# Layer 0: the second half's normalisers in steps inside the first half's attention loop, and state sums row by row

## The chip, the cores and the metric

One core of a Trainium2 chip runs the kernel, a network of four layers, in one launch. The metric is the device time of a run in microseconds. Before the change it was 4101.22 us, the median of three runs (4100.05 to 4104.15).

The engines named below: PE multiplies matrices into PSUM, DVE, ACT and POOL work on vectors, SP issues most of the transfers between SBUF and DRAM. Each of them works through its own queue of instructions in order, and waits for others by semaphores.

## The reference, cut to what matters

Only layer 0 is touched. It is a linear attention over windows of a 64 x 64 image, with 8 heads of 32 channels (d, f below) and three window sizes. `norm` is the normaliser that this change is about: the sum of k over a window, times q, summed over the 32 channels of a head.

```python
q = sigmoid(q); k = sigmoid(k)
v = v / maximum(norm(v, axis=1), 1e-12)
Ik = _integral(k)                       # running sums over rows and columns
Ikv = _integral(einsum('bfhw,bghw->bfghw', k, v))
for w in (1, 2, 4):
    ws = 64 // w
    wk = _box(Ik, ws, 64, 64)           # window sums: four corners of Ik
    wkv = _box(Ikv, ws, 64, 64)
    attn = einsum('bdhw,bdfhw->bfhw', q, wkv)
    norm = einsum('bdhw,bdhw->bhw', q, wk)
    outs.append((attn / (norm[:, None] + 1e-06)).reshape(b, C, 64, 64))
x = x + einsum('bchw,oc->bohw', concatenate(outs, 1), Wout) + bout
```

Layers 1 to 3 (a deformable convolution, a gated linear attention with a mixture of experts, a softmax attention with another) follow and stay as they were.

## The kernel before

The 256 channels are split in two halves of 128 (4 heads each). A tile is 8 x 16 positions (128), 32 tiles in all, 8 rows of 4. Layer 0 has two stages.

**The front** (`layer0`, up to the second group of pools). For each half `hf`: `project0` makes q, k (as 128 channels x 4096), v and, for each tile, the state S = k v; `sums0` adds states of neighbouring tiles on POOL (`near`: rows up to one apart; `S`: up to three rows and one column apart), after all eight rows are there; `norms0` makes the normalisers. `norms0` copies k block by block to `T` (ACT), scans along image rows (DVE), adds down the rows inside a block (7 additions) and from block to block (7), which gives the integral image. Then, for three windows and eight blocks, it makes a product: `d`, a difference of rows of T (DVE), `e`, a difference of columns (a copy on ACT, one or two subtractions on DVE: the middle L433 and the edge L435), and `pr` = e x q (DVE, L437). A matmul with `head_at` sums the channels of each head (L439); all 24 products of a half accumulate into one PSUM bank of 96 rows. At the end DVE takes the reciprocal, and SP stores it to DRAM as `recd`. Tiles `d`, `e`, `prq` have two buffers.

**The loop** (`half0` and `region0`, for both halves one after the other). It computes the attention as masked scores. A half is 224 jobs: for each of two halves of the image 28 jobs for the far tiles, and then for each of four output rows I 4 jobs of the far columns and 12 to 20 near ones. A job is four score matmuls, one per head (L549, into six PSUM banks that are used in turn), whose results are multiplied by a mask and go to SBUF: two heads by DVE (L559), two by ACT (a copy, L555) and POOL (the mask, L565). Two jobs later PE multiplies them with v into accumulators (L592). PE's order in the loop is written out by the program (`manual_schedule`); the order on the other engines is found by a scheduler from the program's dependences.

After a row, `out_rows` multiplies the accumulators by the reciprocals (L616, L628, L629), which were loaded from `recd` over SP with each row broadcast to 32 partitions (L477), projects them (L144, `l_x_ps`) and adds them to x, which was loaded as `xs` (two buffers, L624) and is stored to `xd` (L641). In the first half each row also clears 4160 KB of a list `xs` in DRAM that a later layer uses (`clear_list`: DVE makes zeros, L1553, SP stores them, L1555). `self.later` is a list of small pieces of work, one of which is done per job.

Pools are stacks of memory: the loop's tiles take the space of the front's, so the loop's first instructions wait for the last ones that read the front's tiles.

Of the kernel before, what the change touches and what calls it, by code (L numbers as in the profile page):

```python
# [19 lines left out]
P = 128  # L20
# [66 lines left out]
class Net:  # L87
# [141 lines left out]
    def consts0(self, pool):  # L229
        nc = self.nc  # L230

        self.head_at = pool.tile([P, NBLK, 4 * NBLK], F32, tag="head_at", name="head_at")
        nc.gpsimd.memset(self.head_at, 0.0)
        for h in range(4):
            flat = self.head_at[h * D : (h + 1) * D].rearrange("p a b -> p (a b)")
            nc.gpsimd.memset(flat[:, h : h + 36 * (NBLK - 1) + 1 : 36], 1.0)

        self.gate = pool.tile([P, TR, HW], F32, tag="gate", name="gate")
        nc.gpsimd.memset(self.gate, 1.0)
        nc.gpsimd.memset(self.gate[:, :, 0:1], 0.0)  # L240
# [51 lines left out]
    def layer0(self, xc, x, xd, done):  # L292
# [4 lines left out]
        with tc.tile_pool(name="l0", bufs=1) as pool, tc.tile_pool(name="l0d", bufs=1, space=DRAM) as dpool:  # L297
            q = [pool.tile([P, N], F32, tag=f"q{hf}", name=f"l0_q{hf}") for hf in range(2)]
            k = [pool.tile([P, N], F32, tag=f"k{hf}", name=f"l0_k{hf}") for hf in range(2)]
# [3 lines left out]
            recd = dpool.tile([2, 3 * D, NB], F32, tag="recd", name="l0_recd")  # L303
            with tc.tile_pool(name="l0m", bufs=1) as tmp:
                M = self.masks0(pool, tmp)
            with tc.tile_pool(name="l0y", bufs=1) as ypool:
                self.consts0(ypool)
                y = ypool.tile([P, 2, N], F32, tag="y", name="l0_y")
                tiled = lambda a: a.rearrange("p (i u r c) -> p i r u c", i=NBLK, u=NU, r=TR)
                raster = lambda a: a.rearrange("p (i r u c) -> p i r u c", i=NBLK, r=TR, u=NU)  # L310
                self.group_norm(xc, lambda m: [(tiled(y[:, m])[:, i], raster(xc[:, m])[:, i]) for i in range(NBLK)])
                done()
                with (
                    tc.tile_pool(name="l0g", bufs=1) as gpool,
                    tc.tile_pool(name="l0a", bufs=2) as wp,
                    tc.tile_pool(name="l0a_ps", bufs=2, space=PSUM) as ps,
                ):
                    self.weights(ypool, ["w_qk0", "w_kv0"])
                    for hf in range(2):
                        self.project0(hf, y, q[hf], k[hf], v[hf], S[hf], wp, ps)  # L320
                        self.sums0(S[hf], near[hf], gpool)
                        self.norms0(q[hf], k[hf], recd[hf], gpool, wp, ps)
            with (
# [9 lines left out]
                self.later, self.second = [], []  # L333
                with tc.manual_schedule(engines={mybir.EngineType.PE}):
                    for hf in range(2):
                        self.half0(hf, q[hf], k[hf], v[hf], S[hf], near[hf], recd[hf], M, bd, x, xd, st, wp, ps)
                    for go in self.second:
                        go()
                    while self.later:
                        self.later.pop(0)()  # L340
# [4 lines left out]
    def project0(self, hf, y, q, k, v, S, wp, ps):  # L345

        nc, w = self.nc, self.w
# [7 lines left out]
        for nb in range(NBLK):  # L355
# [24 lines left out]
            for h in range(4):  # L380
                hp = slice(h * D, (h + 1) * D)
                (nc.scalar.copy if h % 2 else nc.vector.tensor_copy)(S[hp, ts, :], p[hp, :, hp])

    def sums0(self, S, near, pool):


        nc = self.nc
        I8 = lambda a: a.rearrange("p (i j) e -> p i j e", j=4)
        R = pool.tile([P, NT, D], F32, tag="R", name="l0_R")
        f32, r, s4 = I8(near), I8(R), I8(S)  # L390
        add = lambda o, a: nc.gpsimd.tensor_tensor(o, o, a, ALU.add)
        nc.gpsimd.tensor_copy(near, S)
        add(f32[:, 1:], s4[:, :-1])
        add(f32[:, :-1], s4[:, 1:])
        nc.gpsimd.tensor_copy(R, near)
        for d in (2, 3):
            add(r[:, d:], s4[:, :-d])
            add(r[:, :-d], s4[:, d:])
        nc.gpsimd.tensor_copy(S, R)
        add(s4[:, :, 1:], r[:, :, :-1])  # L400
        add(s4[:, :, :-1], r[:, :, 1:])

    def norms0(self, q, k, recd, pool, wp, ps):
# [3 lines left out]
        T = pool.tile([P, HW + 1, HW], F32, tag="T", name="l0_T")  # L407
        nc.gpsimd.memset(T[:, 0, :], 0.0)
        k5 = k.rearrange("p (i u r c) -> p i r u c", i=NBLK, u=NU, r=TR)
        flat = lambda a: a.rearrange("p r x -> p (r x)")  # L410
        rows = T[:, 1:].rearrange("p (i r) x -> p i r x", r=TR)
        for i in range(NBLK):
            nc.scalar.copy(rows[:, i].rearrange("p r (u c) -> p r u c", c=HC), k5[:, i])
            nc.vector.tensor_tensor_scan(flat(rows[:, i]), flat(self.gate), flat(rows[:, i]), 0.0, ALU.mult, ALU.add)
        add = lambda o, a: nc.vector.tensor_tensor(o, o, a, ALU.add)
        for r in range(1, TR):
            add(rows[:, :, r], rows[:, :, r - 1])
        for i in range(1, NBLK):
            add(rows[:, i], bc(rows[:, i - 1, TR - 1], 1, TR))
        p = ps.tile([P, NB], F32, tag="nrm", name="l0_nrm_ps", bufs=1)  # L420
        for wi, ws in enumerate(WINS):
            half, ni = ws // 2, ws // 2 // TR
            a, b = half + 1, HW - half + 1
            for i in range(NBLK):

                d = T[:, TR * (i + ni) : TR * (i + ni + 1)] if i + ni < NBLK else bc(T[:, HW], 1, TR)
                if i >= ni:
                    hi, d = d, wp.tile([P, TR, HW], F32, tag="d", name="l0_d")
                    nc.vector.tensor_tensor(d, hi, T[:, TR * (i - ni) : TR * (i - ni + 1)], ALU.subtract)
                e = wp.tile([P, TR, HW], F32, tag="e", name="l0_e")  # L430
                nc.scalar.copy(e[:, :, :a], d[:, :, half - 1 : half - 1 + a])
                if b > a:
                    nc.vector.tensor_tensor(e[:, :, a:b], d[:, :, a + half - 1 : b + half - 1], d[:, :, a - half - 1 : b - half - 1], ALU.subtract)  # L433
                at = max(a, b)
                nc.vector.tensor_tensor(e[:, :, at:], bc(d[:, :, HW - 1], 2, HW - at), d[:, :, at - half - 1 : HW - half - 1], ALU.subtract)  # L435
                pr = wp.tile([P, NU, TR, HC], F32, tag="prq", name="l0_prq")
                nc.vector.tensor_tensor(pr.rearrange("p u r c -> p r u c"), e.rearrange("p r (u c) -> p r u c", c=HC),  # L437
                                        q[:, i * NB : (i + 1) * NB].rearrange("p (u r c) -> p r u c", u=NU, r=TR), ALU.mult)
                nc.tensor.matmul(p[wi * D : (wi + 1) * D, :], self.head_at[:, i, :], pr.rearrange("p u r c -> p (u r c)"),  # L439
                                 start=(i == 0), stop=(i == NBLK - 1))  # L440
        rec = pool.tile([3 * D, NB], F32, tag="rec", name="l0_rec")
        nc.vector.tensor_scalar_add(rec, p[: 3 * D], 1e-6)
        nc.vector.reciprocal(rec, rec)
        nc.sync.dma_start(out=recd, in_=rec)
# [85 lines left out]
    def region0(self, full, jobs, k, v, wp, ps, after):  # L530
# [68 lines left out]
        for i in range(len(jobs)):  # L599
            done = first(i)  # L600
            if self.later:
                self.later.pop(0)()
            self.second.append((lambda i, done: lambda: second(i, *done))(i, done))
# [3 lines left out]
    def out_rows(self, hf, I, accs, o64, rcp, x, xd, st, wp, ps, part):  # L607
# [13 lines left out]
        if part == 0:  # L621
            self.xs0 = wp.tile([P, 2, NB], F32, tag="xs", name="l0_xs")
# [1585 lines left out]
```

## Time and profile before

| | |
|---|---|
| median of the runs | 4101.22 us (4100.05 to 4104.15) |
| the profiled execution | 4099.97 us, of which its span is 4098.3 |
| mean granted PE clock | 0.927 of full speed |
| busy over the whole span | PE 87%, DVE 42%, ACT 31%, POOL 35% |
| front of layer 0 (first projection to first mask) | 29.1 to 263.5 us |
| first half's loop, to about | 700 us |
| second half's loop, to about | 1055 us |
| the other layers | 1055 to 4098 us |

In the stage of 263.5 to 1055 us PE is busy for 780.24 us of 791.5. In layers 1 to 3 nothing is changed. The page names L565 (POOL, 769.9 us over the two layers that use such lines), L559 (DVE, 492.2) and L555 (ACT, 367.5) as its costliest groups; these are the masks of the loop.

A busy engine is not always the one that sets the end, so the views to read are: busy time by stage; in a stage, what the busiest engine waits for; and the timeline around the place in question.

### The profile page before, as it was taken

Reading aid. Unit: us, or ns where it says so; the run is one execution under the profiler, and the core shown is the slowest. Engines: PE = TensorE matmul, PEld = TensorE weight load, DVE = VectorE, ACT = ScalarE, POOL = GpSimd, SP = SyncE. Lnnn points to the kernel's source line nnn. Section 1 sums busy time; section 2 is a strip of 40 time slices with the busy share of each in tenths; the row PEclk is TensorE's granted clock in tenths of the full one; section 3 lists DMA queues with packets and bytes.
Section 4 is the critical chain, followed back from the end, with each engine's and each line's share of the span. In section 5 each row is a group of like instructions: output and inputs, shape, how many; then the busy total and the mean of one; then the engine's idle time right before and its main releaser. Section 6 shows DMA issues by size and latency. Waiting matters only on the chain.

```text
span 4098.3 us, 57080 instructions
## 1 busy us (share of the span) xinstructions
PE 3563.3 (87%) x21872; PEld 2338.6 (57%) x21872; DVE 1738.9 (42%) x4404; ACT 1267.3 (31%) x2588; POOL 1445.4 (35%) x1376
## 2 busy tenths in 40 slices
PE   7879999999977767656678797999999999799997
PEld 4423433333335656544456575666666668688886
DVE  6876656565653554556566557011011101211111
ACT  4424343434423535311112234122222212233331
POOL 1258898888952243433334341000000001111110
PEclk9989999999998978878778798999999999899999
DMA  1003414210023111110001484000000000455554
GB/s 52 2 26 109 126 57 136 58 39 33 26 94 109 51 44 49 44 30 0 1 11 43 137 259 145 0 10 1 11 11 11 11 11 14 167 193 192 191 190 174
DMA packets 137792, 294.09 MB, mean 72 GB/s; under 512 B 14817, under 2 KB 72802, under 8 KB 128290
## 3 DMA queue, kind: packets, MB, share of 16 engines
q1 hardware_dynamic: 113138, 234.80, 17.7%
q0 software_dynamic: 13056, 35.93, 2.3%
q10 hardware_dynamic: 11312, 19.55, 1.4%
q8 instruction: 178, 2.92, 0.3%
q14 instruction: 108, 0.88, 0.1%
HBM read 202.53 MB, written 87.70 MB: 71 GB/s over the span
## 4 chain that ended last, share of the span: by engine, by line
PE 35%; issue 11%; DVE 5%; POOL 3%; DMA 2%; ACT 1%; SPq 0%; ACTq 0%; POOLq 0%; DVEq 0%
PE a_o_ps L1945 11%; PE a_s_ps L144 11%; PE f_h_ps L144 2%; PE a_qkv_ps L144 2%; PE f_y_ps L144 2%; POOL ys L1782 2%; DMA ys<-f_y,f_at 1%; PE a_q_ps L144 1%; DVE a_sm L1309 1%; PE tr_ps L217 1%; DMA f_g<-ys 1%; PE a_o_ps L144 1%; PE a_u_ps L144 1%; PE a_c_ps L1334 1%; POOL a_tmp L1165 0%
## 5 line engine op out<-in xcount | busy, mean ns | idle before, releaser
L565 POOL TENSOR_TENSOR l_sm<-l_sc,mask 128x512 f32<-128x512 f32 (+3 forms) x624 | 769.9, 1268 | 119.5 <-ACT l_sc L555 117.4
L559 DVE TENSOR_TENSOR l_sm<-l_s,mask 128x256 f32<-128x256 f32 (+3 forms) x1248 | 492.2, 447 | 302.7 <-PE l_s L549 292.9
L555 ACT COPY l_sc<-l_s 128x384 f32<-128x384 f32 (+3 forms) x896 | 367.5, 461 | 558.9 <-PE l_s L549 537.1
L1945 PE MATMUL a_o_ps<-a_v,a_e 128*128 128x257 f32 x2048 | 489.2, 380 | 0.0
L144 PE MATMUL a_s_ps<-a_qT,a_nT 128*128 128x512 f32 (+1 forms) x1152 | 487.8, 546 | 0.0
L1945 PEld LDWEIGHTS a_o_ps<-a_v,a_e 128*128 128x128 f32 x2048 | 388.9, 190 | 147.0 <-issue 103.8
L549 PE MATMUL l_s<-l_q,l_k 32*128 32x384 f32 (+2 forms) x3584 | 423.8, 514 | 7.1 <-ACT l_sc L555 4.1
L1641 POOL DMA_INDIRECT xs<-f_n,f_to x64 | 62.4, 975 | 883.6 <-DVE f_to L1638 840.9
L1940 ACT ACTIVATE a_e<-a_s_ps 128x512 f32<-128x512 f32 (+1 forms) x288 | 158.0, 549 | 687.3 <-PE a_s_ps L144 687.2
L144 PE MATMUL f_h_ps<-f_xT,f_w 128*128 128x256 f32 x1440 | 344.1, 387 | 15.2 <-ACT f_h L1755 5.5
L1782 POOL DMA_INDIRECT ys<-f_y,f_at x144 | 139.6, 970 | 571.3 <-ACT f_y L1781 545.4
L144 PE MATMUL f_y_ps<-f_w,f_h 128*128 128x256 f32 x1440 | 328.1, 379 | 0.0
L144 PEld LDWEIGHTS f_h_ps<-f_xT,f_w 128*128 128x128 f32 x1440 | 264.8, 191 | 83.7 <-ACT f_h L1755 31.5
L854 PE MATMUL l_acc_ps<-ident,l_pr 128*128 128x128 f32 x1600 | 208.9, 291 | 117.8 <-DVE l_pr L850 114.1
L549 PEld LDWEIGHTS l_s<-l_q,l_k 32*128 32x128 f32 x3584 | 164.6, 183 | 240.6 <-issue 123.2
L144 PEld LDWEIGHTS a_s_ps<-a_qT,a_nT 128*128 128x128 f32 x1152 | 216.3, 190 | 129.9 <-issue 112.9
L144 PEld LDWEIGHTS f_y_ps<-f_w,f_h 128*128 128x128 f32 x1440 | 268.2, 190 | 33.7
L854 PEld LDWEIGHTS l_acc_ps<-ident,l_pr 128*128 128x128 f32 x1600 | 193.8, 151 | 132.7 <-DVE l_pr L850 126.4
L850 DVE TENSOR_TENSOR l_pr<-l_vk,l_w_ps 128x1280 f32<-128x1280 f32 x128 | 182.1, 1480 | 91.0 <-ACT l_w_ps L839 79.8
L1755 ACT ACTIVATE f_h<-f_h_ps,f_w 128x256 f32<-128x256 f32 x360 | 163.7, 468 | 131.9 <-PE f_h_ps L144 131.9
L592 PE MATMUL l_a_ps<-l_sm,l_v 128*32 128x512 f32 (+3 forms) x1408 | 179.0, 530 | 1.6 <-POOL l_sm L565 1.5
L592 PE MATMUL l_b_ps<-l_sm,l_v 128*32 128x256 f32 (+2 forms) x2176 | 172.4, 376 | 0.5 <-POOL l_sm L565 0.5
(441 smaller groups left out, 4357.6 us busy)
## 6 DMA issues: line engine op xcount, KB each, us to landing
f_w<-in_f_w SPq DMA_DIRECT2D x36, 1152.0 KB
f_w<-in_f_w SPq DMA_DIRECT2D x36, 1028.0 KB
xs<-zero SPq DMA_DIRECT2D x8, 4160.0 KB
l_vk<-vt SPq DMA_DIRECT2D x180, 128.0 KB
f_x<-xs SPq DMA_DIRECT2D x72, 260.0 KB
f_w<-in_f_w SPq DMA_DIRECT2D x36, 384.0 KB
l_rcp<-l_recd SPq DMA_DIRECT2D x48, 256.0 KB
f_w<-in_f_w SPq DMA_DIRECT2D x36, 257.0 KB
```

What stands on the lines that cost most here:

```text
L144: self.nc.tensor.matmul(out, lhsT, rhs, start=(i == 0), stop=(i == len(pairs) - 1))
L549: nc.tensor.matmul(s[pair, j], k[hp, key * P : (key + 1) * P], qs[hp], start=True, stop=True)
L555: nc.scalar.copy(sc[:, j], s[1, j])
L559: nc.vector.tensor_tensor(sms[0][:, j, at : at + t * wide].rearrange("p (t n) -> p t n", n=wide), part[:, which, :], mask, ALU.mult)
L565: nc.gpsimd.tensor_tensor(sms[1][:, :, at : at + t * wide].rearrange("p j (t n) -> p j t n", n=wide), part[:, :, which, :], bc(mask, 1, 2) ...
L592: nc.tensor.matmul(out, v[:, key, hp], sms[pair][:, j, base + lo * wide : base + hi * wide], start=not seen[nm], stop=(left[nm] == 0 and h ...
L850: nc.vector.tensor_tensor(pr, vk, bc(wps[:, j, dy], 3, D), ALU.mult)
L854: nc.tensor.matmul(acc[:, m, j, :], pf[:, dx, m * P : (m + 1) * P], self.ident, is_transpose=True, start=(j == 0 and dy == 0 and dx == 0 a ...
L1755: nc.scalar.activation(h[:, m, :], q, AF.Gelu, bias=w1[:, 2 * hidden + m : 2 * hidden + m + 1])
L1782: nc.gpsimd.indirect_dma_start(out=self.ys_parts[(i % 4) * NI + k], in_=y[:, k, :], in_offset=None, out_offset=bass.IndirectOffsetOnAxis(a ...
L1940: nc.scalar.activation(e, p, AF.Exp, scale=1.0 / 16.0)
L1945: nc.tensor.matmul(o[i][:, : C + 1], e[:, i * P : (i + 1) * P], v[:, j, :], start=(j == 0), stop=(j == NT - 1))
```

## The change

Four things are done together.

- `norms0` becomes a list of steps: 8 scans, 14 additions, 25 steps that each finish one product (`total`) and make the next (`product`), and `invert`. For half 0 all of them are called in the front. For half 1 the eight scans are called in the front; the other steps are called from `region0` in the loop, one every fourth job, and two more after them.
- Half 1's T takes the place of its k (`kz`): k is copied to DRAM (`kd`) first and loaded again at the end of the steps.
- The head sum of a product is no longer accumulated over 24 products in one bank: each goes to 4 rows of its own bank (in the loop one of the six banks of the scores), is copied back into the first four rows of `pr` by ACT and stored to DRAM (`sumd`) by SP. `invert` loads all 96 rows, takes the reciprocal and stores it. `d`, `e` and `prq` have one buffer each, as has `xs` of the loop. The gate of the scan is bf16 and 128 x 512.
- `sums0` is called after each row of states, and adds what that row completes.

Its core as a diff:

```diff
@@ layer0
+            kz = pool.tile([P, HW + N], F32, tag="kz", name="l0_kz")
+            k = [pool.tile([P, N], F32, tag="k0", name="l0_k0"), kz[:, HW:]]
...
                     for hf in range(2):
-                        self.project0(hf, y, q[hf], k[hf], v[hf], S[hf], wp, ps)
-                        self.sums0(S[hf], near[hf], gpool)
-                        self.norms0(q[hf], k[hf], recd[hf], gpool, wp, ps)
+                        self.project0(hf, y, q[hf], k[hf], v[hf], S[hf], near[hf], gpool, wp, ps)
+                        if hf == 0:
+                            T = gpool.tile([P, HW + N], F32, tag="T", name="l0_T")
+                            for go in self.norms0(q[0], k[0], T, sumd[0], recd[0], wp, lambda: ps.tile([P, NB], F32, tag="nrm", name="l0_nrm_ps", bufs=1)):
+                                go()
+                        else:
+                            nc.sync.dma_start(out=kd, in_=k[1])
+                            for go in self.norms0(q[1], k[1], kz, sumd[1], recd[1], wp, None)[:NBLK]:
+                                go()
...
+                self.slow = self.norms0(q[1], k[1], kz, sumd[1], recd[1], wp,
+                                        lambda: ps.tile([P, 4, P], F32, tag="s", name="l0_nrm_ps", bufs=6).rearrange("p a b -> p (a b)"))[NBLK:]
+                self.slow.append(lambda: nc.sync.dma_start(out=k[1], in_=kd))
+                self.turn = 0
@@ project0, after the states of block nb
+            self.sums0(nb, S, near, R)
@@ sums0, for row I
+        add(near[:, I], S[:, I], S[:, I - 1])
+        add(near[:, I - 1], near[:, I - 1], S[:, I])
+        lo = max(0, I - 3)
+        add(R[:, lo:I], R[:, lo:I], bc(S[:, I], 1, I - lo))
...
+        if I >= 3:
+            done = slice(I - 3, I - 2) if I < NBLK - 1 else slice(I - 3, NBLK)
+            nc.gpsimd.tensor_copy(S[:, done], R[:, done])
+            add(S[:, done, 1:], S[:, done, 1:], R[:, done, :-1])
+            add(S[:, done, :-1], S[:, done, :-1], R[:, done, 1:])
@@ norms0
+        room = lambda nm: wp.tile([P, TR, HW], F32, tag=nm, name=f"l0_{nm}", bufs=1)
+        def scan(i):
...
+            e = room("e")
+            nc.scalar.copy(e.rearrange("p r (u c) -> p r u c", c=HC), k5[:, i])
...
+            nc.vector.tensor_tensor_scan(flat(rows[:, i]), self.gate, flat(e), 0.0, ALU.mult, ALU.add)
...
+        def total(wi, i):
+            p, pr = bank(), made["pr"]
+            nc.tensor.matmul(p[:4], self.head_of, pr, start=True, stop=True)
+            nc.scalar.copy(pr[:4], p[:4])
+            nc.sync.dma_start(out=sumd[wi * D + 4 * i : wi * D + 4 * i + 4, :], in_=pr[:4])
+
+        def invert():
+            rec = room("d").rearrange("p r x -> p (r x)")[: 3 * D]
+            nc.sync.dma_start(out=rec, in_=sumd)
+            nc.vector.tensor_scalar_add(rec, rec, 1e-6)
+            nc.vector.reciprocal(rec, rec)
+            nc.sync.dma_start(out=recd, in_=rec)
+
+        steps = [call(scan, i) for i in range(NBLK)]
+        steps += [call(down, r) for r in range(1, TR)] + [call(carry, i) for i in range(1, NBLK)]
+        todo = [(wi, i) for wi in range(len(WINS)) for i in range(NBLK)]
+        for prev, nxt in zip([None] + todo, todo + [None]):
+            steps.append(call(lambda prev, nxt: [prev and total(*prev), nxt and product(*nxt)], prev, nxt))
+        return steps + [invert]
@@ region0, after the first part of each job
+            self.turn += 1
+            if self.slow and self.turn % 4 == 0:
+                self.slow.pop(0)()
@@ out_rows
-            self.xs0 = wp.tile([P, 2, NB], F32, tag="xs", name="l0_xs")
+            self.xs0 = wp.tile([P, 2, NB], F32, tag="xs", name="l0_xs", bufs=1)
```

`down` and `carry` are the additions of before, and `product` makes `d`, `e` and `pr` with the same instructions as before.

## The prediction

> **What bounds the kernel now.** I first read the page's slices and a table of windows, which cut layer 0 off at 1055 us and split it in a front (29.1 to 263.5: projections, running sums, normalisers) and the two halves of the attention loop. Columns: window; busy us of PE, weight loads, DVE, ACT, POOL; granted clock; DMA share; GB/s.
>
> ```profile
> 29.10:175.00 145.90, 133.55 (x415) 69.00 (x416) 111.79 (x195) 75.08 (x157) 21.13 (x13) 0.96 0.01 2
> 175.00:258.00 83.00, 57.79 (x195) 28.21 (x194) 74.50 (x139) 34.90 (x80) 20.49 (x11) 0.84 0.00 1
> 218.00:241.00 23.00, 7.12 (x9) 0.87 (x10) 23.00 (x19) 1.51 (x5) 20.49 (x11) 0.60 0.00 1
> 263.50:700.00 436.50, 428.48 (x4229) 166.98 (x4230) 266.14 (x629) 178.24 (x430) 382.95 (x370) 0.99 0.35 99
> 398.70:588.00 189.30, 187.24 (x1816) 71.09 (x1812) 114.48 (x263) 78.26 (x189) 163.60 (x150) 1.00 0.34 96
> 420.00:436.00 16.00, 15.90 (x194) 6.78 (x194) 11.11 (x35) 7.56 (x21) 15.07 (x16) 1.00 1.01 275
> ```
>
> The front is bound by PE until about 175 (134 of 146 us) and by DVE after it: DVE makes the second half's normalisers alone. The loop is bound by PE (98% busy); DVE is busy 61% and POOL 88%. So work taken off the end of the front is worth its time, and what goes into the loop costs all of what it puts on PE.
>
> Next the timeline of DVE and POOL inside the first half's state sums, for what one does to the other:
>
> ```profile
> 109.95 0.42 DVE L433 TENSOR_TENSOR l_e<-l_d 128x256 f32<-128x256 f32 x1
> ...
> 113.99 4.62 POOL L391 TENSOR_TENSOR l_near<-l_near,l_S 128x896 f32<-128x896 f32 x2
> 114.38 2.30 DVE L433 TENSOR_TENSOR l_e<-l_d 128x256 f32<-128x256 f32 x1
> 116.60 2.15 DVE L435 TENSOR_TENSOR l_e<-l_d 128x120 f32<-128x120 f32 x1
> ```
>
> The same difference takes 0.42 us alone and 2.30 beside POOL: each ends just after a POOL instruction ends. DVE instructions with two SBUF operands wait for POOL's running instruction, and the next one for the next.
>
> Then the front's end, and the groups of POOL and DVE in the loop:
>
> ```profile
> 255.42 0.69 DVE L437 TENSOR_TENSOR l_prq<-l_e,l_q 128x512 f32<-128x512 f32 x1 [0.48 <-DVE l_e L435]
> 256.16 1.05 PE L439 MATMUL l_nrm_ps<-l_prq,head_at 128*32 128x512 f32 x2 [0.73 <-DVE l_prq L437]
> 257.97 3.35 DVE L443 RECIPROCAL l_rec<-l_rec 96x512 f32<-96x512 f32 x1
> 261.35 0.32 SPq L444 DMA_DIRECT2D l_recd<-l_rec  x1
> 263.50 1.07 ACT L555 COPY l_sc<-l_s 128x512 f32<-128x512 f32 x2 [9.41 <-DMA l_recd<-l_rec]
> ```
> ```profile
> L565 POOL TENSOR_TENSOR l_sm<-l_sc,mask 128x512 f32<-128x512 f32 x110 | 124.8, 1158 | 14.2 <-ACT l_sc L555 14.2
> L1553 DVE TENSOR_SCALAR zero<-l_o 128x260 int32<-128x260 int32 x7 | 10.4, 1492 | 0.2
> ```
> ```profile
> 419.60 0.58 SPq L1555 DMA_DIRECT2D xs<-zero  x1
> ```
>
> A store and its landing cost 2.15 us (261.35 to 263.50). The loop already has a DVE instruction held up by POOL: the zeroing takes 1.49 us on average and 0.30 at best. And the clear of xs (4160 KB, one per output row in the first half) keeps all DMA engines full for some 15.5 us (419.6 to about 435; share 1.01).
>
> **The change part by part.** In the instruction order of the two built programs, the changed one has half 0's 24 products in the front, half 1's eight scans at its end, and half 1's 14 additions in the loop's jobs 0 to 4 (not one per four jobs). Its 24 head sums stand on PE at every fourth job from 64 to 156, and each product follows one job behind.
>
> *The front.* Each product now has one buffer, and its rows go out by PE, ACT and a store before the next product may be written: 0.69 (L437) + 1.05 (L439) + 0.60 (a 128x512 PSUM copy on ACT, L467) + 2.15 (store) + some 0.2 of hand-overs = 4.7 us per product, against 1.8 between products at 241 to 254. While projections remain, PE's order puts enough of them between two head sums to hide this. 16 head sums stand there, 8 behind. PE's front work without head sums is 133.55 + 57.79 - 54.6 = 136.7; 16 at 1.05 add 16.8; at 95% busy (133.55/145.9 is 92% with DVE's waits) that ends at 29.1 + 153.5/0.95 = 191. Eight chained products follow at 4.7 to 5.6 us (the head sum took 1.9 where the clock stood at 0.60), say 5.0: 231. Behind the last product, as DVE's order has it: six scans with one buffer (copy 0.62 + scan 1.21 + 0.1, each 1.93: 11.6), the addition 0.7, the reciprocal 3.35, two more scans (3.2) and a down addition: 20 us. The last product stands 1.2 us before its sum's end, so the loop starts at 230 + 20 = 250 instead of 263.5: 13.5 us gained. Bounds: 33 (every chain 4.2 us, PE at 98%) and 0 (chains at 5.6, PE at 92%). The copy of k to DRAM (2 MB) sits between two head-sum stores; at 275 GB/s it holds the next back 7.6 us, inside the 5% idle.
>
> State sums: POOL does the same additions in eight portions. Half 1's old ones ended by 239.3, 24 us before the loop; hidden behind the projections, they cost nothing. If that cover went, the last row (about a fifth of 20.5 us) would come at the end: 4 us. The bf16 gate, the small constants, and one buffer for xs (its load waits for a store 35 us before use) cost nothing for the same reason.
>
> *The loop, on PE.* 24 head sums of two 512-column passes: 24 x 0.97 (1.05 less overlap) = 23 us, on the engine that is 98% busy.
>
> *The loop's first jobs.* 14 additions of 0.68, two edges, a product and a difference (2.2): 11.7 us of DVE in jobs that start up with DVE idle for half the time (6.95 of 18.5 us busy from 263.5): 8 us, between 4 (all in idle time) and 14 (each also waits for POOL).
>
> *The loop's steps, on DVE.* From job 64 to 156 (398.7 to 588, found by counting score matmuls) PE needs 189.3 + 23 = 212. DVE has 114.5. The products add 23 of 24 times their sum: edges 7.0, middles 7.8, products 16.3, differences 17 x 0.68 = 11.6, together 42.7 uncontended, so 41. Of these, 62 instructions (23 edges, 23 products, 16 middles) meet POOL, which is busy 86%; the mean POOL instruction is 1.29 us. Each waits between half of one (0.65 x 0.7 = 0.45) and a whole one (1.29); I take 0.9, nearer the whole one, since in the front sums each waited a whole one: 56. The differences did not wait there. Then the product waits for its store: the head sum starts, 3.85 us later the store has landed (1.05 + 0.6 + 2.15 + hand-over); DVE reaches the product one job later, after 2.1 to 2.9 us. So 1.2 us x 20 = 24. Sum 114.5 + 41 + 56 + 24 = 235.5, 23 over PE's 212. DVE also can't use the 10.8 us that it sits behind the output projection (waits in its queue for l_x_ps): 34 us. What waits behind DVE is l_sm, then PE's next score matmul, whose bank it must empty: PE has under one job of slack. Bounds: 0 (0.45 and 0.5 us) and 64 (1.29 and 1.5).
>
> *The clears.* Stores of SP go out behind the clear. Three clears fall where a product needs a store: issued at 419.6, 468.5 and 573.0, done 15.5 later, and PE's head sums at jobs 76, 100 and 152 (426.4, 475 and about 580) stand behind the product. No row shows a small store behind a clear. Lower bound 0 (it goes beside it), upper bound the clear's rest: 9 + 9 + 9, and 6 more at the last, where the 2 MB reload of k (7.6 us) is put ahead: 33. As all DMA engines are full, I take the upper end less 3 us of waits counted already: 30. [...]
>
> *The end.* The reciprocal (3.35) and its wait for the reloaded sums in DVE's queue: 4 us (2 to 8).
>
> Sum: -13.5 + 23 + 8 + 34 + 30 + 4 = +85.5. The profiled execution took 4099.97 us, span 4098.3 and 1.7 around it; the median of the runs is 4101.22, so 4187.
>
> **The rivals.** *A, DVE's idle time takes the steps in (faster).* For it: DVE is idle 170 us in the half, and the part moved is some 55 us. If the front's chain runs at 4.7 from the first product (80 us) on, the last stands at 80 + 23 x 4.7 = 188 and the loop starts at 208: 55 gained; the loop pays the 23 on PE and 5: 4074. Against it: PE's order places 16 head sums behind projections, and PE's slack is under a job. It decides where a step delays DVE by less than 1.8 us. *B, stores overtake the clears:* 4187 - 30 = 4157. For it: a store is only 8 KB. *C, every contended instruction waits a whole POOL one, and stores land later:* +64 for +34, +14 for +8, nothing gained in the front: 4101 + 85.5 + 30 + 6 + 13.5 = 4236. *D, nothing to see:* front at its best (33), DVE steps free, no clears: -33 + 23 + 4 + 2 = -4: 4097. That the steps are not moved is excluded by the order.
>
> **How the numbers follow.** Forecast 0.46, B 0.18, C 0.18 (a part of it beyond 4255), A 0.14, D 0.04. The likeliest alone is 4165 to 4210. The range goes from D's 4097 to 4255, C with some lower clock. Below 4093 (0.2%, about what this measurement can tell from no change): 0.14; within: 0.04; above: 0.82.
>
> **What would show it.** Loop start near 250; eight head sums some 5 us apart before it; L433, L435 and L437's successors at over 1 us in the loop; PE in the first half's loop below 90%; DVE waiting for the store of l_prq, over 5 us at three places. Wrong if DVE's waits on that store are short, or if the loop starts before 225.

## The result, and the profile after

The changed kernel takes 4197.4 us (median of four runs, 4193.8 to 4206.9), the kernel before 4100.8 beside it: a ratio of 1.0238, 95% interval 1.022 to 1.0255. It is slower by 96.6 us; 4187 was predicted. The profiled execution has a span of 4195.0 us and a mean granted clock of 0.918 (before: 4098.3 and 0.927).

A correction first. The text before the prediction says that the first half's loop ends at about 700 us and the second's at about 1055. In the trace of the kernel before, the last addition of a row to x (its start is what is called a row's end below) stands at 743.65 for the first half and at 1204.59 for the second:

```profile
743.65 0.69 DVE L637 TENSOR_TENSOR l_xs<-l_xs,l_x_ps 128x512 f32<-128x512 f32 x1 [1.50 <-PE l_x_ps L144]
...
1204.59 0.69 DVE L637 TENSOR_TENSOR l_xs<-l_xs,l_x_ps 128x512 f32<-128x512 f32 x1 [1.61 <-PE l_x_ps L144]
```

No term of the predicted sum rests on the wrong figures. Rival A's 170 us of idle DVE does (188 by the right end), and so do the loop lengths in one expectation below.

Row ends locate the loss. Us from the span's start, or lengths between; the start is the first copy of a score by ACT.

| | before | after | longer |
|---|---|---|---|
| start of the loop | 263.50 | 241.33 | -22.2 |
| start to end of row I=0 | 105.8 | 113.2 | +7.4 |
| I=0 to I=1 | 42.7 | 44.3 | +1.6 |
| I=1 to I=2 | 48.9 | 71.0 | +22.1 |
| I=2 to I=3 | 48.6 | 72.8 | +24.3 |
| I=3 to I=4 (the lower far jobs lie here) | 106.0 | 172.4 | +66.4 |
| I=4 to the end of row I=7 | 128.2 | 128.2 | 0.0 |

The sum is +99.6; in the whole span 96.7 of it is left. The table of windows of the kernel after says what the bad stretches look like (columns as in the prediction's first fence: window; busy us of PE, weight loads, DVE, ACT, POOL; granted clock; DMA share; GB/s):

```profile
175.00:242.00 67.00, 28.48 (x66) 7.62 (x65) 40.96 (x63) 20.93 (x46) 16.99 (x27) 0.56 0.02 7
399.00:470.00 71.00, 56.26 (x524) 21.64 (x520) 42.94 (x97) 24.60 (x60) 45.78 (x40) 0.90 0.31 88
543.00:715.00 172.00, 133.66 (x1004) 44.31 (x996) 100.50 (x172) 55.62 (x128) 98.42 (x81) 0.84 0.18 51
715.00:844.00 129.00, 126.48 (x1317) 51.55 (x1316) 82.98 (x206) 48.42 (x120) 110.01 (x109) 1.00 0.51 143
```

PE, 98% busy in the loop of before, is busy 79% and 78% in the second and third line, and no other engine is over 65%: nobody is full, everybody waits. Behind the last step (fourth line) all is as before.

The front's tail, from the timeline of the kernel after (start, us, engine, line, operation; in brackets the idle time before it and what ended it):

```profile
203.48 0.69 DVE L467 TENSOR_TENSOR l_prq<-l_e,l_q 128x512 f32<-128x512 f32 x1 [2.49 <-DMA l_sumd<-l_prq]
...
204.23 1.87 PE L473 MATMUL l_nrm_ps<-l_prq,head_of 128*4 128x512 f32 x2 [2.83 <-DVE l_prq L467]
...
206.13 0.57 ACT L474 COPY l_prq<-l_nrm_ps 4x512 f32<-4x512 f32 x1 [1.66 <-PE l_nrm_ps L473]
208.19 0.69 DVE L467 TENSOR_TENSOR l_prq<-l_e,l_q 128x512 f32<-128x512 f32 x1 [2.14 <-DMA l_sumd<-l_prq]
```

Product, head sum, copy, store, next product: 4.7 us a turn, and DVE waits for the store.

The loop's waits, between 250 and 760 us (engine, line, what ended the wait: total us, times, longest):

```profile
PE l_nrm_ps L473 <- DVE l_prq L467: 40.7, 3, 16.1
DVE l_prq L467 <- DMA l_sumd<-l_prq: 35.7, 3, 14.4
PE l_s L595 <- DVE l_sm L605: 21.6, 11, 4.6
```

Three long waits of DVE for a store become three of PE. The last of them in the timeline:

```profile
644.05 0.35 SPq L346 DMA_DIRECT2D l_kz<-l_kd  x1
646.81 0.59 SPq L1604 DMA_DIRECT2D xs<-zero  x1
...
648.61 0.59 PE L473 MATMUL l_nrm_ps<-l_prq,head_of 128*4 128x512 f32 x1
...
650.26 12.82 SPq L475 DMA_DIRECT2D l_sumd<-l_prq  x1
670.66 0.69 DVE L467 TENSOR_TENSOR l_prq<-l_e,l_q 128x512 f32<-128x512 f32 x1 [14.42 <-DMA l_sumd<-l_prq]
```

SP has issued the reload of k (2 MB) and the clear (4160 KB); the 8 KB store behind them starts to be issued at 650.26, and the product that needs its tile free starts at 670.66, after a wait of 14.42 us. The issue alone lasts 12.82 us here (8.93 and 8.95 behind the other two clears), where one with no clear ahead of it lasts 0.24; from its end to the product it is another 7.5 to 7.8 us at all three places, and 1.2 in the front's tail.

The third line of the waits points at the other loss. DVE's groups in the loop of the kernel after, 240 to 760 us (count | busy us, mean ns | idle before):

```profile
L467 DVE TENSOR_TENSOR l_prq<-l_e,l_q 128x512 f32<-128x512 f32 x24 | 23.6, 981 | 35.7 <-DMA l_sumd<-l_prq 35.7
L459 DVE TENSOR_TENSOR l_d<-l_kz 128x512 f32<-128x512 f32 x17 | 20.1, 1182 | 0.9
L465 DVE TENSOR_TENSOR l_e<-l_d 128x56 f32<-128x56 f32 x7 | 9.8, 1393 | 0.0
```

The edge of 56 columns takes 0.20 us alone and 1.39 here; the contiguous difference 0.68 and 1.18. One step in full, among the far jobs:

```profile
623.73 0.68 DVE L467 TENSOR_TENSOR l_prq<-l_e,l_q 128x512 f32<-128x512 f32 x1
...
624.93 0.55 DVE L463 TENSOR_TENSOR l_e<-l_d 128x384 f32<-128x384 f32 x1
625.32 4.22 POOL L611 TENSOR_TENSOR l_sm<-l_sc,mask 128x1024 f32<-128x1024 f32 x2 [2.00 <-ACT l_sc L601]
625.39 2.15 DVE L465 TENSOR_TENSOR l_e<-l_d 128x56 f32<-128x56 f32 x1
...
627.64 2.45 DVE L459 TENSOR_TENSOR l_d<-l_kz 128x512 f32<-128x512 f32 x1
...
630.75 1.01 PE L595 MATMUL l_s<-l_q,l_k 32*128 32x384 f32 x2 [3.74 <-DVE l_sm L605]
```

POOL's two masks run from 625.32 to 629.54. DVE's edge ends as the first does (627.5), the difference 0.55 us after the second; the next score mask stands behind both, and PE, whose bank that mask empties, idles 3.74 us.

### The profile page after: what moved, and what is told of

Same layout as the page of the kernel before. It is cut to its first block, busy times and chain, and to the rows that moved or that the text cites. A ratio compares the mean times of both kernels' runs of the same rounds, so it can differ in the third digit from the quotient of the medians.

```text
span 4195.0 us, 57405 instructions
## 1 busy us (share of the span) xinstructions
PE 3585.6 (85%) x21872; PEld 2343.2 (56%) x21872; DVE 1754.8 (42%) x4404; ACT 1298.2 (31%) x2638; POOL 1482.2 (35%) x1454
## 4 chain that ended last, share of the span: by engine, by line
PE 34%; issue 12%; DVE 5%; POOL 2%; DMA 1%; ACT 1%; POOLq 0%; SPq 0%; ACTq 0%; DVEq 0%
PE a_o_ps L1994 11%; PE a_s_ps L144 11%; PE f_h_ps L144 2%; PE a_qkv_ps L144 2%; POOL ys L1831 2%; PE f_y_ps L144 2%; PE a_q_ps L144 1%; DMA f_g<-ys 1%; PE tr_ps L217 1%; DVE a_sm L1358 1%; PE a_o_ps L144 1%; PE a_u_ps L144 1%; PE a_c_ps L1383 1%; POOL a_tmp L1214 0%; PE f_r_ps L144 0%
## 5 line engine op out<-in xcount | busy, mean ns | idle before, releaser
L611 POOL TENSOR_TENSOR l_sm<-l_sc,mask 128x512 f32<-128x512 f32 (+3 forms) x624 | 780.4, 1286 | 221.7 <-ACT l_sc L601 218.8
L605 DVE TENSOR_TENSOR l_sm<-l_s,mask 128x256 f32<-128x256 f32 (+3 forms) x1248 | 493.0, 447 | 304.9 <-PE l_s L595 298.7
L595 PE MATMUL l_s<-l_q,l_k 32*128 32x384 f32 (+3 forms) x1792 | 241.7, 538 | 35.5 <-DVE l_sm L605 22.0
L595 PE MATMUL l_s<-l_q,l_kz 32*128 32x384 f32 (+3 forms) x1792 | 209.1, 512 | 0.0
L638 PE MATMUL l_a_ps<-l_sm,l_v 128*32 128x512 f32 (+3 forms) x1408 | 188.5, 547 | 5.3 <-POOL l_sm L611 5.2
L595 PEld LDWEIGHTS l_s<-l_q,l_k 32*128 32x128 f32 x1792 | 92.8, 192 | 175.3 <-issue 65.5
```

The costliest lines, as they stand in the source:

```text
L595: nc.tensor.matmul(s[pair, j], k[hp, key * P : (key + 1) * P], qs[hp], start=True, stop=True)
L605: nc.vector.tensor_tensor(sms[0][:, j, at : at + t * wide].rearrange("p (t n) -> p t n", n=wide), part[:, which, :], mask, ALU.mult)
L611: nc.gpsimd.tensor_tensor(sms[1][:, :, at : at + t * wide].rearrange("p j (t n) -> p j t n", n=wide), part[:, :, which, :], bc(mask, 1, 2) ...
L638: nc.tensor.matmul(out, v[:, key, hp], sms[pair][:, j, base + lo * wide : base + hi * wide], start=not seen[nm], stop=(left[nm] == 0 and h ...
```

## The experiments

The theory: four things set the time, namely a shorter front, PE's head sums, DVE's products (dear where POOL holds them up), and stores behind the clears. Rivals: DVE's idle time takes the products in; stores pass the clears; one buffer for `xs`, the copy of k or other small parts cost what the products seem to. The kernel before was run again beside each group of runs; "us" below is the median, and the ratio is to that kernel before.

| run | us | ratio, 95% interval |
|---|---|---|
| e1_clears_second | 4161.7 | 1.0146 (1.0129 to 1.0163) |
| e3_act_stores | 4176.0 | 1.0183 (1.0166 to 1.02) |
| e4_all_front | 4214.2 | one run; before 4102.0 |
| e7_row_sums_alone | 4088.7 | 0.9968 (0.9958 to 0.9977) |
| e5_no_products | 4108.8 | 1.0014 (1.0005 to 1.0024) |
| e6_double_sums | 4191.1 | 1.0214 (1.0196 to 1.0231) |
| e8_pool_split | 4154.6 | 1.0123 (1.0106 to 1.014) |
| e9_near_only | 4163.8 | 1.0149 (1.0132 to 1.0166) |
| e10_front_two | 4158.3 | 1.0077 (1.006 to 1.0094) |
| e11_near_fourth | 4181.8 | 1.0137 (1.0116 to 1.0158) |
| e12_no_pool_mask | 4129.0 | 1.0065 (1.0049 to 1.0082) |
| e13_before_no_pool | 4095.9 | 0.9983 (0.9974 to 0.9993) |

Beside e10 and e11 the kernel before took 4128.1, beside the others 4102 to 4103; for those two the ratio is to be read, not the time.

**The clears moved away.** The changed kernel, with the clears of `xs` in the second half:

```diff
-            if hf == 0:
+            if hf == 1:
                 self.clear_list(I, o[:, 0, :], wp)
```

> The clears of the list are issued in the second half's rows instead of the first's, where no step runs. Theory 1 (stores of the head sums wait behind the clears, the product behind the store on DVE, the head sum behind the product on PE): the three waits of DVE for the store, 35.7 us in the changed kernel, go, and the time falls from 4197 to 4160-4168. Rival (the engine is late anyway, the waits only move): 4185 or more.

35.7 us less than the changed kernel. The waits view of this kernel, 250 to 760 us:

```profile
DVE l_prq L467 <- DMA l_sumd<-l_prq: 5.0, 3, 3.1
```

The wait for the store falls from 35.7 to 5.0 us, so stores don't pass the clear on SP's queue; and without clears this wait is all but gone: 20 of the 23 products never show it. From the end of row I=0 to that of I=4 the loop grows over before by 78.1 us in place of 114.3.

**The small stores on another queue.**

```diff
-            nc.sync.dma_start(out=sumd[...], in_=pr[:4])
+            nc.scalar.dma_start(out=sumd[...], in_=pr[:4])
```

> The stores of the head sums are issued from ACT's queue instead of SP's; the clears stay where they were. If a small store is held by the order of SP's own queue, the three waits shrink to a few us each and the time is 4163-4175. If it is held because all DMA engines are full of the clear's packets, whatever queue it comes from, the waits stay near 36 us and the time is 4190-4205.

Between the two. Waits view, 250 to 760 us:

```profile
DVE l_prq L467 <- DMA l_sumd<-l_prq: 21.6, 9, 5.8
```

21.4 us less than the changed kernel, 7.9 of it in the front (start at 233.43: there the products stand closer together beside the projections, the fourth at 98.78 in place of 108.49; why isn't shown). The longest wait falls from 14.4 to 5.8 us and the sum from 35.7 to 21.6, and from row I=0 to I=4 the loop is 17.3 us shorter than in the changed kernel, where e1 gains 36.3. So the order in SP's queue was about half of it. A store from the other queue still waits beside a clear (in the kernel before the DMA share was 1.01 from 420 to 436 us, during one): waits of 5.3, 5.8 and 4.8 us end 8.7 to 9.5 us after a clear was issued. The issue of such a store now lasts 0.25 us, and from its end to the product it is still 5.8 to 6.8 us.

**The row sums alone.** The kernel before, with `sums0` after each row of states and nothing else of the change.

> The kernel before with only the state sums row by row. Theory 1 (a product of DVE waits for each POOL instruction it meets; before the change four products in each half took 5.8 us instead of 1.8, 16 us at the end of the front): half 1's sums now lie beside projections and few products, and the front is 8-18 us shorter: 4083-4093. Rival (as many waits in smaller portions): 4098-4106.

Faster than before; of the versions that leave nothing out it is the only one. Its loop starts 12.3 us earlier (251.24); the time gains 13.3. That part of the change is a gain by itself.

**All of the second half's steps in the front**, with the same single buffers, banks and copy of k; no step in the loop.

```diff
-                self.slow = self.norms0(q[1], k[1], kz, sumd[1], recd[1], wp, ...)[NBLK:]
+                self.slow = []
```

> All steps of the second half in the front again, each still with one buffer and its own bank and store; the loop has none. Theory 1: the loop from first to last mask takes 791-795 us as before the change (it took about 913 with the steps), so one buffer for xs and the rest cost it nothing; the front grows by 24 products at 4.7 us, 14 additions and a second reciprocal, some 130 us: loop start near 372, time near 4212. Rival (the loop is slower for other reasons than the steps, such as xs or the bank that they take): the loop stays above 820 us.

The loop starts at 379.36, and from there each row ends as far behind the start as before (the row ends shift by 116, as the start does). So one buffer for `xs`, the new matrices and the copy of k cost the loop nothing: what the loop lost came with the steps. The expectation's lengths of 791-795 and 913 us, and the rival's limit of 820, go with the wrong end of 1055; from the start to the last row's end the loop takes 941.1 us before, 941.5 here and 1063.1 in the changed kernel.

**Without the products.** On the kernel with the clears moved; of the loop's products only the first is made, the head sums, copies and stores of all stay (of part of the normalisers the values are thus not computed).

```diff
         def product(wi, i):
+            if bank is self.loop_bank and made:
+                return
```

> On e1 (4161.7): of half 1's 24 products in the loop only the first is made on DVE; the head sums, copies and stores stay (the second half's normalisers are not the reference's). Theory 1 (DVE's instructions with two SBUF operands wait for POOL and stand ahead of the masks): what is left over the front's gain is the additions (8), the head sums on PE (24) and the end (4): 4105-4118. Rival 2 (the head sums on PE with their bank out of the six of the scores cost most): above 4135.

52.9 us less than with them. By row ends, I=0 to I=4 grows by 14.1 us in place of 78.1, so the products cost 64.0 there; behind the last row this profiled execution took 7 us longer than that of e1 (2900.4 against 2893.0), in code that is the same, so the times show less. The 14.1 are all that head sums, copies, stores and the reciprocal cost where no product stands beside them. From row I=3 to I=4, where eleven of the head sums and the reciprocal lie, the stretch takes 115.5 us, 9.5 more than before:

```profile
499.17:614.66 115.49, 112.68 (x1006) 39.80 (x1007) 64.65 (x136) 53.19 (x119) 95.58 (x81) 0.97 0.07 21
```

**Each head sum twice**, also with the clears moved:

```diff
-            nc.tensor.matmul(p[:4], self.head_of, pr, start=True, stop=True)
+            for _ in range(2 if self.in_loop else 1):
+                nc.tensor.matmul(p[:4], self.head_of, pr, start=True, stop=True)
```

> On e1 (4161.7): each head sum of the loop is made twice in the same bank. If PE sets the pace, the second costs what the first does, 24 x 0.97 us: 4182-4190. If PE has room while DVE is late (rival: the head sums are hidden in the stalls), under 4172.

+29.4 us, a little over the expectation; from row I=0 to I=4 +21.2, 0.9 us for each of 24, where 0.97 was expected. The second sums on PE cost nearly their full time.

**POOL's long masks in two halves**, from job 110 to the last step:

```diff
-                nc.gpsimd.tensor_tensor(sms[1][:, :, ...], part[:, :, which, :], bc(mask, 1, 2), ALU.mult)
+                    for j in range(2):
+                        nc.gpsimd.tensor_tensor(sms[1][:, j, ...], part[:, j, which, :], mask, ALU.mult)
```

> On e1 (4161.7): from job 110 to the last step, POOL's mask is applied in two instructions of half the size where a job is of the far kind. Theory 1 (an instruction of DVE waits for the whole running instruction of POOL): in the far jobs the 128x56 edge falls from 1.6 us towards 0.9, the differences likewise, and 7 far steps give back some 1.5-3 us each: 4140-4152. Rival (the waits of DVE have another cause, such as ACT's copy or the store): 4158-4166, with the edge at its 1.6.

A part only: -7 us, which the intervals of the two ratios don't tell from none; by row ends the stretch from I=3 to I=4 falls from 162.8 to 150.7. The edge of 56 columns fell from 1.52 to 0.72 us, but the 384-column middle rose from 0.86 to 0.97, and POOL was busy 109.5 us in place of 99.3 from row I=3 to I=4.

**POOL's masks left out**, from job 110 to the last step, 40 of them; and the kernel before with the same 40 left out.

```diff
+            bare = bool(self.slow) and len(outs) == 1 and self.turn >= 110 and outs[0][1] == P and ns[0] == n
...
-                nc.scalar.copy(sc[:, j], s[1, j])
+                nc.scalar.copy(sms[1][:, j].rearrange(...)[:, :n] if bare else sc[:, j], s[1, j])
...
-            for (_, wide, which, _, _, mask), t in zip(outs, ns):
+            for (_, wide, which, _, _, mask), t in zip([] if bare else outs, ns):
```

> The change with the clears moved to the second half (4161.7, ratio 1.0146), and from job 110 to the last step POOL does no mask where a job has one full 4-tile part (40 masks of 1024 elements left out; ACT's copy of the scores goes to the place of their result unmasked, so that part of the computation is left out). The steps, their head sums and their stores stay. The stretch from the end of row I=3 to the end of row I=4 grew by 56.8 us over the kernel before. If what a step costs there is the time that DVE waits for POOL's running mask: edges and differences take 0.2 and 0.7 us instead of 1.6, the stretch grows by 15 to 30, the ratio is 1.005 to 1.009. If it costs the same whether DVE waits for POOL or not (DVE's own 1.8 us per product, the head sum and the chain of hand-overs): the stretch grows by 42 or more and the ratio is 1.011 to 1.0145.

> The kernel before with the same 40 masks of POOL left out (unmasked copies in their place) and nothing else: what leaving them out is worth by itself. The stretch from row I=3 to I=4 is bound by PE there (98% busy): both theories expect no change beyond 2 us in it, and a ratio of 0.998 to 1.001. A gain of over 5 us would have to be taken off what e12_no_pool_mask shows.

DVE's groups, 505 to 680 us, first of the kernel with the clears moved, then of this one:

```profile
L459 DVE TENSOR_TENSOR l_d<-l_kz 128x512 f32<-128x512 f32 x8 | 12.1, 1510 | 0.6
L465 DVE TENSOR_TENSOR l_e<-l_d 128x56 f32<-128x56 f32 x7 | 10.6, 1518 | 0.0
```
```profile
L459 DVE TENSOR_TENSOR l_d<-l_kz 128x512 f32<-128x512 f32 x8 | 5.5, 689 | 0.6
L465 DVE TENSOR_TENSOR l_e<-l_d 128x56 f32<-128x56 f32 x7 | 1.5, 220 | 0.0
```

Both are back at their uncontended times. The stretch from row I=3 to I=4 in the tables of windows, in the kernel before, with the clears moved, without POOL's masks, and in the control:

```profile
509.51:615.50 105.99, 105.28 (x984) 37.64 (x985) 61.15 (x136) 46.98 (x108) 94.99 (x81) 1.00 0.20 59
```
```profile
514.41:677.22 162.81, 136.97 (x1006) 45.39 (x1008) 103.01 (x171) 55.68 (x128) 99.26 (x81) 0.86 0.08 28
```
```profile
514.47:644.30 129.83, 122.16 (x1006) 42.83 (x1008) 80.21 (x171) 55.70 (x128) 36.17 (x44) 0.95 0.10 35
```
```profile
508.37:609.60 101.23, 100.53 (x984) 36.16 (x987) 61.02 (x135) 47.01 (x108) 34.53 (x44) 1.00 0.22 62
```

Leaving the masks out is worth 4.8 us by itself (101.23 against 105.99 in before; the control's expectation said at most 2), and 33.0 with the steps there. So some 28 of the 56.8 us that this stretch had grown were DVE waiting for POOL, and what followed from it. The steps occupy DVE for 45.0 us with the masks and 23.1 without them, and PE's waits for DVE's masks in the stretch all but go (first with the clears moved, then without POOL's masks):

```profile
PE l_s L595 <- DVE l_sm L605: 23.6, 8, 4.6
```
```profile
PE l_s L595 <- DVE l_sm L607: 2.8, 4, 1.6
```

With the clears moved, PE waits nowhere in this stretch for a mask of POOL, so POOL being late itself is no rival. The other 28.6 us (129.83 - 101.23) are there without any wait for POOL, for 10 products, their head sums and the reciprocal. Both inputs of the edge and of the difference lie in SBUF: with POOL's masks they took 1.52 and 1.51 us, without them 0.22 and 0.69. In the kernel after, from 240 to 760 us, the 14 products (L467) that began while an instruction of POOL ran took 0.77 to 2.65 us and ended 0.54 or 0.55 us behind its end, the other ten 0.68 or 0.69; the zeroing (L1602), with one input in SBUF, took 1.62 to 1.70 us where POOL ran and 0.30 where it did not; the score masks of 512 columns (L605), which read PSUM and SBUF, took 0.67 to 0.69 us in both cases. So the prediction's "two SBUF operands" does not name all that was held up.

**Other places for the steps.** With the clears moved, the steps only beside near jobs: every third of them, then every fourth.

```diff
-            self.turn += 1
-            if self.slow and self.turn % 4 == 0:
+            if self.slow and far_jobs and len(self.slow) > 27:
                 self.slow.pop(0)()
+            elif self.slow and not far_jobs:
+                self.turn += 1
+                if self.turn % 3 == 0:
+                    self.slow.pop(0)()
```

> On e1 (4161.7): the 14 additions go with the first far jobs, the other steps with every third job of rows 0 to 3, none with the far jobs of the lower image half, where POOL's instructions are longest (up to 2.13 us against 1.16). Theory 1: in e1 a step cost about 1.6 us in rows 2 and 3 and over 5 among the far jobs, so seven or eight dear steps become cheap ones: 4125-4142. Rival (a step costs the same wherever it stands, or more at three jobs than at four): 4155-4175.

> e9_near_only with one change: a step with every fourth near job in place of every third (fewer steps per row, more rows). e9 was 4163.8, the clears-moved kernel 4161.7. If the close spacing was what made e9's steps dear: 4130 to 4145, and rows I=0 to I=2 grow by a third or more less each per step. If a step costs about the same wherever it stands, because PE has no slack for what DVE is held up: 4155 to 4168.

The first missed: 4163.8, as much as with the far jobs. From row I=0 to I=2, 15 products lengthen the two stretches by 57.8 us (3.9 each); at every fourth job 17 products lengthen three by 41.8 (2.5 each). In layer 0 that saves 14.5 us (last row's end 1252.9 against 1267.4), as the theory of spacing has it; but the ratios, 1.0149 and 1.0137, don't tell the two apart, and beside a kernel before of 4102 us e11 would take 4158, not 4130 to 4145. These figures also mix kinds of products. The first eight (window 64) have no middle, and four of them no difference; six of the twelve in e1's cheap rows are of that kind, and none of the ten among its far jobs, so e9's comparison of cheap and dear places was in part one of cheap and dear products. Of the later kinds, products 14 to 21 cost 3.8 us each at every third job (e9, I=1 to I=2), and 10 to 21 cost 2.9 at every fourth (e11, I=1 to I=3). That a step costs less far from the last one is seen in the rows; that it pays in the time isn't shown.

**Two buffers for the product in the front**, with the clears moved:

```diff
-            pr = wp.tile([P, NU, TR, HC], F32, tag="prq", name="l0_prq", bufs=1)
+            pr = wp.tile([P, NU, TR, HC], F32, tag="prq", name="l0_prq", bufs=self.prq_bufs)
```

> The change with the clears moved to the second half, and in the front a second buffer for the product (prq), so that a product need not wait for the store of the one before it; the loop keeps one buffer. If the one buffer sets the front's tail (after's products are 4.7 us apart there, DVE waiting 2.1 to 2.5 for the store): the eight products come about 2.4 to 3.2 us apart, the loop starts 12 to 19 us earlier (about 225 to 230 instead of 242), and the time is 4143 to 4151 (4161.7 less that). If something else spaces them (DVE's own 1.8 us per product at the low clock, the running sums queued behind): loop start 236 or later, 4156 to 4164.

More than expected: the ratio falls from 1.0146 to 1.0077, some 28 us. The loop starts at 215.60, 25.2 earlier than with one buffer (240.81), and the last row of layer 0 ends 34.0 earlier. Its timeline (start, us):

```profile
206.64 2.05 PE L144 MATMUL l_S_ps<-l_v,l_kt 128*128 128x128 f32 x8 [4.77 <-DVE l_v L393]
...
213.50 2.06 POOL L407 TENSOR_TENSOR l_S<-l_S,l_R 128x384 f32<-128x384 f32 x2
215.60 0.59 ACT L603 COPY l_sc<-l_s 128x512 f32<-128x512 f32 x1 [5.70 <-POOL l_S L407]
```

No tail of products is left: they run beside the projections, the last of them at 164.44, and what the loop now waits for is the last row of state sums on POOL. The second half's 14 additions have moved into the front as well (190.4 to 205), and the stretch from the start to the end of row I=0 takes 106.4 us, against 112.2 with one buffer and 105.8 before.

## Why the prediction came out where it did

The sign was right, and so were the three costs that the prediction named (PE's head sums, DVE's steps, the stores behind the clears). That 4187 came so near to 4197 is in part luck: the term for DVE's steps was 30 us too small, and those for the front and the head sums, 22 us too large together, hid most of it. By its steps, row ends first (they add up to the 99.6 of the table), then the times:

| term | predicted | by row ends | by times |
|---|---|---|---|
| front | -13.5 | -22.2 | |
| first jobs | +8 | +7.4 | |
| head sums and end | +27 | +14.1 (e5) | +29.4 for a second set (e6) |
| DVE steps | +34 | +64.0 (e1 less e5) | +52.9 |
| clears | +30 | +36.3 (after less e1) | +35.7 |
| sum | +85.5 | +99.6 | +96.6 (after less before) |

How the loop's 78.1 us divide between head sums and DVE steps depends on which is taken away first: by e6's price of 21.2 for the head sums, 57 would be left for DVE's steps, still 23 more than predicted.

- *Front.* The turn was 4.7 us as worked out, where I took 5.0, and seven turns stood in the tail (189.26 to 222.34), where I had eight; so the last product stood at 222.34, where I had 230. The 20 us behind it were 19.0. What I did not see is that one buffer made the whole tail: e10 removes it.
- *First jobs.* Right, and e10 bears it out: with the additions in the front, 0.6 of the 7.4 is left.
- *Head sums.* Their 23 us is right as a price of PE work (e6: 21.2 by row ends), but without the products they cost less: 14.1 with the end's reciprocal.
- *DVE steps*, the term that failed: 34 predicted, 64.0 measured. The products were to take 42.7 alone and 56 more behind POOL. DVE's groups in the loop after add up to 74.2 for L459, L463, L465 and L467, so 31.5 more: the 56-column edges waited 1.2 us on average, about half of POOL's 2.1 us for a far mask, and the near jobs' edges of 120 columns hardly at all (0.34 in place of 0.27). "The differences did not wait there" was wrong: they waited 0.5 us on average. Ordinary store waits were to cost 24; they cost 5.0 in e1. So DVE's load was some 45 us smaller than I made it, and still it cost 30 us more.

  The step that failed: "Sum [...] 235.5, 23 over PE's 212", which lets all of DVE's idle time but 10.8 us be used. It can't be. In the stretch from row I=3 to I=4 the kernel without products (e5) takes 9.5 us more than before, and DVE is busy for only 64.65 of its 115.5. Take these 9.5 off, on the assumption that the two costs add. Then products that occupy DVE for 40.9 us (e1, summed from its timeline, without the reciprocal) lengthen the stretch by 47.3, and products that occupy it for 18.9 us (e12) lengthen it by 19.1 over the control. Each microsecond of a product costs about one, the lower clock included. The timeline at 623.73 shows how: the score masks queue behind the step, and PE has too little finished work ahead.
- *Clears.* 30 predicted at three places, 35.7 measured at three places; the 3 us I took off for waits counted already were not there to be counted. What the lower clock behind these stalls (0.90 in 399 to 470 us) adds isn't separated.
- *Rivals.* A (DVE's idle time takes the steps in) is refuted by e5 and e12. B (stores overtake) by e1, and for another queue by half in e3. C had the front wrong (nothing gained), but its 64 for DVE's steps and 36 for the clears are what was measured; the reason it gave for the 64 is not the one found, since the instructions did not each wait a whole one of POOL's. D is excluded by the result.

What was to be seen: start near 250 (241), head sums 5 us apart (4.7), PE in the first half's loop below 90% (87% of the whole, 78 and 79% in the bad stretches), waits for the store of over 5 us at three places (10.5, 10.8 and 14.4). Of the three lines that were to take over 1 us, only one did, and in one form: the edge of 56 columns (L465, 1.39); the middle (L463, 0.62 and 0.86 in its two main forms, once 1.40) and the product (L467, 0.98) stayed under it. The difference (L459), which was not named, took 1.18.

The best version is e7, 0.32% faster than before. What stays open: whether the head sums' 9.5 us and the products' 19.1 in the far stretch simply add, what the kind of a product, its place and its spacing are each worth, and whether wider spacing still would bring the steps in the loop below e7. None of these was tried by itself.

## What to carry to other kernels

The idle share of an engine in a pipeline where each job waits for the last was not room for other work here: price every microsecond put into its queue at a microsecond of the loop until a run shows otherwise, and more beside a busy POOL (the edge of 56 columns took 1.52 us with POOL's masks, 0.22 without). A small store that something waits for didn't belong behind a bulk store on one queue here (35.7 us of waits, 5.0 with the clears elsewhere). And in a chain through DRAM the second buffer can be worth the whole tail: 25 us at the loop's start here, some 28 in the time.

## What the runs showed of the hardware

Behind a stall of 3.90 us in the middle of the loop the granted clock was 0.50 for 6.8 us, so the stall cost more than its length. In the timeline of the kernel after, a stall, and two jobs' score matmuls behind it:

```profile
613.90 2.08 PE L595 MATMUL l_s<-l_q,l_k 32*128 32x512 f32 x4 [3.90 <-DVE l_sm L605]
...
617.77 2.09 PE L595 MATMUL l_s<-l_q,l_k 32*128 32x512 f32 x8
...
621.96 1.14 PE L595 MATMUL l_s<-l_q,l_k 32*128 32x512 f32 x8
```

The same eight records take 2.09 us and then 1.14. The granted clock was 0.50 from 613.7 to 620.5 and full behind that (table of windows):

```profile
613.70:620.50 6.80, 6.60 (x24) 1.43 (x28) 2.65 (x6) 1.11 (x3) 2.13 (x1) 0.50 0.01 2
620.50:626.00 5.50, 5.50 (x42) 1.16 (x34) 3.56 (x7) 3.18 (x8) 2.80 (x2) 1.00 0.01 1
```

In the stretch from I=3 to I=4 PE's 1006 matmuls are busy 136.97 us at a clock of 0.86 (e1) and 122.16 at 0.95 (e12), though the work is the same: of the 33 us between those stretches PE is busy for 15. In e9 the same six matmuls took nearly twice the time at one place as 8 us later:

```profile
420.64 5.49 PE L144 MATMUL l_x_ps<-l_o,w_out 128*128 128x512 f32 x6 [0.44 <-DVE l_o L682]
...
428.73 2.84 PE L144 MATMUL l_x_ps<-l_o,w_out 128*128 128x512 f32 x6
```

Six output projections took 5.49 us and then 2.84. From 396 us to the first line that execution shows no stall of PE over 1.9 us (the longest took 1.82), so here no stall as long as the 3.90 us stood ahead of the slow ones. What lowers the clock isn't shown.
